# A gated delta-rule memory beside an FFN: crossing the halves for n = 1, and separate PSUM banks

## The chip, the core and the metric

The kernel runs on one core of a Trainium2 chip. The metric is the device time of one execution in microseconds, the median of the runs. A NeuronCore has a matrix engine (TensorE, PE in the profile; its weight loads are PEld), VectorE (DVE), ScalarE (ACT), GpSimd (POOL) and SyncE (SP), which here issues all DMAs. Each works through its own queue in order.

## The reference

The input x has shape [4, 2048, 256]: four batch elements, 2048 tokens, 256 features. A conditioning vector gives, per batch element, two shifts, two scales and two gates (adaLN). Two blocks follow:

```python
h = _layernorm(x) * (1 + ca) + sa
x = x + ga * attn(h)          # gated delta-rule memory, 4 heads of 64, chunks of 64 tokens
h = _layernorm(x) * (1 + cb) + sb
x = x + gb * ffn(h)           # silu(h W1) * (h W2), two GELU layers of 1024, back to 256
```

The memory of a head is a 64x64 state S. For each chunk, with A the inverse of a unit triangular 64x64 matrix that the chunk's keys give:

```python
v_new = A_i @ v_i - (A_i @ wk_i) @ S
o_i = rkg_i @ S + intra_i @ v_new
S = gamma_C * S + wkg_i @ v_new
```

The memory's output is `h + (alpha * o) @ Wr.T`.

## The kernel before

A step is one chunk of 64 tokens of all four batch elements, numbered 2n + b; there are 32 steps. With tokens on partitions, b takes the partitions 64b to 64b + 63 and n lies along the free axis. With features on partitions, head 2p + h takes the partitions 64h to 64h + 63. So the memory's products come in 16 units (p, n, h, b) of 64x64x64, and each of them occupies a 64x64 quarter of the matrix engine: the row half is the partition half of its operands, the column half that of its output.

The FFN of a step runs beside the recurrence of the next step and the chunk's own matrices of the one after that. Its products (line 431) are 128x128 by 256: 128 for the gated layers, 256 for the two hidden layers (16 chunks of 128 outputs, 16 products each), 32 for the last layer. Each activation is kept as two parts, whose sum is exact: `act` is first rounded by ScalarE (L367), and then the residue is computed by VectorE (hidden layers) or GpSimd (gated layers), both L368.

The memory's work in one step, as the matrix engine does it:

- `rec_state` (L305) has two groups of products with the state: R (L310), which is subtracted from v to give `rem`, and O (L314), the part of the memory's output that comes from the state. O stays open in PSUM until `rec_update`.
- the last layer of the FFN (`last`), then the next step's gated layers, and among them the transpositions `tp` (L200);
- `local_grams` (L230): G, the products of keys, masked by VectorE into NMT and IT (L242, L243). NMT's diagonal blocks of 32 go to DRAM (d1) and come back as U in another layout; VectorE inverts them row by row (`local_inverse`, zt and Z, L258 and L260), and `local_blocks` (L263) stores Z to DRAM (d2) and loads it into E by four DMAs; VectorE transposes the blocks into Dm (L271).
- `local_merge1` and `local_merge2` (yp L280, ep L293) complete the inverse E from its blocks of 32;
- `rec_values` (L321): V = E times rem; `rec_update` (L330): IT times vn is added onto the open O in PSUM (L337), SS (L342) updates the state; ScalarE copies O to oT (L345);
- `rec_out` (L353): oT times wrT, the output projection.

The write keys wkg are loaded by two to four DMAs that follow E's loads in SyncE's queue, and GpSimd scales them (L214).

[...] three for the FFN (`pf`), two tiles of two banks each for `ps2`, one for `ps1`. In `ps2` live tp, G, R, O and SS, in `ps1` vp, yp, ep, V, the output projection and a transposition.

The order of each engine's queue is set by a planner that runs through the program with its own estimate of every instruction's duration, and takes what is ready first, what is emitted earlier first. `tc.issue_after` puts the memory's products behind a given FFN product: after the q-th chunk of the hidden layers (`steps`, L658 to L708). The two hidden layers' chunks, q = 0 to 15, are thus the rail along which everything else is placed. The inverse of step s + 2 is spread over these chunks, and `local_blocks` and `rec_state` follow after the 16th.

Set-up (L470 to L646) loads and rounds the weights, compares them with what was rounded (L526, L528), and works out the first matrices. `held` and `after` delay instructions there behind marked ones.

Of the kernel before, what the change touches and what calls it, by code (L numbers as in the profile page):

```python
# [35 lines left out]
# Columns of the constants: what stays, then what only the set-up needs.  # L36
IDENT, UNIT = 0, 128
KEPT = 128 + 8 * K
# [4 lines left out]
def constants():  # L43
    """By the shapes alone: indices and masks over the positions of a tile."""
# [5 lines left out]
    # Row 4 * n + (partition // 32) of the identity.  # L50
    unit = np.zeros((P, 8, K), np.float32)
    for n in range(8):
        unit[i, n, 4 * n + i // K] = 1.0
    out[:, UNIT:UNIT + 8 * K] = unit.reshape(P, -1)
# [7 lines left out]
def over(ap, dim, n):  # L62
    """`ap` with a dimension of n that repeats it."""
    shape = list(ap.shape)
    shape.insert(dim, n)
    return ap.unsqueeze(dim).to_broadcast(shape)
# [3 lines left out]
def adaln_block_kernel(ctx: ExitStack, tc: tile.TileContext, x_in, ww, wr, decay, log_alpha, w1, w2, h1, h2, w3, scol,  # L70
# [17 lines left out]
    kept = cp.tile([P, KEPT], F32, name="kept")  # L88
    ident = kept[:, IDENT:IDENT + P]
    unit = kept[:, UNIT:UNIT + 8 * K].rearrange("q (c i) -> q c i", i=K)  # L90
    wwT = cp.tile([P, NK, D], F32, name="wwT")
    wrT = cp.tile([P, NK, D], F32, name="wrT")
# [47 lines left out]
    def after(name):  # L140
        """What follows is issued behind what was marked last, on its engine."""
        return tc.issue_after(mark[name])
# [15 lines left out]
    def moments(x):  # L158
        """The mean of each token, and one over its deviation."""
# [34 lines left out]
    def local_keys(s, first=False):  # L194
# [7 lines left out]
        nc.scalar.copy(hT, tp[:, 0])  # L202
# [6 lines left out]
        # The write keys, a token behind, with tokens on partitions.  # L209
# [20 lines left out]
    def local_grams(s):  # L230
        IT, NMT = ITs[s % 2], NMTs[s % 2]
        # The heads h are row tiles, each with a bank of its own.
# [18 lines left out]
        nc.gpsimd.tensor_scalar(Z, unit, 1.0, None, ALU.mult)  # L251

    def local_inverse(s, j0, j1):
        """Rows of the inverse of the diagonal blocks of 32: partition (g, block, unit), row 4 * c + g at c."""
# [8 lines left out]
    def local_blocks(s):  # L263
        dst = d2.rearrange("(c g) x u i -> g (x u) c i", g=4)
        for g in range(4):
            move(out=dst[g], in_=Z[K * g:K * g + K])
        for b in range(2):
            for k in range(2):
                r = slice(C * b + K * k, C * b + K * k + K)
                move(out=E[r, :, K * k:K * k + K], in_=d2[:, 2 * b + k])  # L270
        nc.vector.transpose(Dm, E[:, :, 0:K])  # L271

    # E = [[EA, EA NMT EB], [0, EB]], of the blocks of 32.
    def local_merge1(s):
        NMT = NMTs[s % 2]
        yp = ps1.tile([P, 8, K], F32, tag="a1", name="yp")
        for u in range(8):
            for b in range(2):
                a = C * b
# [462 lines left out]
```

## Time and profile before

| | |
|---|---|
| median of three runs | 1785.5 us (1785.21 to 1786.7) |
| span of the profiled execution | 1783.4 us |
| mean granted TensorE clock | 0.983 |
| length of a steady step | 52.5 us |
| busy, PE / DVE / ACT / POOL | 97% / 65% / 55% / 34% |
| products of the FFN (L431), busy | 1024.8 + 256.2 + 126.8 us |
| V (L325), O from the state (L314), busy | 37.6 us (x1024), 36.4 us (x992) |
| R (L310), G (L239), O from vn (L337), SS (L342), busy | 22.3, 22.7, 22.7, 21.1 us |
| yp (L280), ep (L293), busy | 22.2, 22.6 us |

The page gives the span of one profiled execution, from its first to its last instruction, and no other time of that execution; the runs' median is 2.1 us above it. Busy times of a group leave out overlaps. Instructions of the matrix engine are pipelined: the time that one costs the engine is best read from when the next one starts. An fp32 product leaves two records, so 16 units are "x32". In a timeline a row is: start in us, busy us, engine, line, operation, output <- inputs, shapes, count, and in brackets the idle time before it and what ended it. SPq rows are the DMA issues of SyncE.

### The profile page before, as it was taken

To read this page: it belongs to the slowest core of one execution; us is meant where nothing else is said; L and a number is where in the kernel's file an instruction comes from. 1 tells how busy PE (TensorE), PEld (TensorE's weight loads), DVE (VectorE), ACT (ScalarE), POOL (GpSimd) and SP (SyncE) were. 2 spreads that over 40 slices of the span, in tenths; PEclk is the share of its full clock that TensorE was granted. 3 is DMA by queue.
4 is the path that set the end of the run, shared out by engine and by line. 5 is a ranking of instruction groups with operands and counts; after the bars stand their busy time and mean duration, and the time that the engine had idled before them with its cause. 6 is when DMAs were issued, how large, how long until landed. Compare 5 with 4: busy or idle time off the path is not lost.

```text
span 1783.4 us, 49902 instructions
## 1 busy us (share of the span) xinstructions
PE 1724.5 (97%) x20372; PEld 1653.5 (93%) x20372; DVE 1162.4 (65%) x3705; ACT 984.0 (55%) x2254; POOL 615.2 (34%) x615
## 2 busy tenths in 40 slices
PE   6489999999999999999999999999999999999998
PEld 3279999999999999999999999999999999999998
DVE  6876767666767666677766667766667776566532
ACT  6245555565555556555656655555655565565554
POOL 3234323334433334442323443333343232344111
PEclk8689999999999999999999999999999999999999
DMA  8311111111111111111111111111111111111100
GB/s 278 98 40 38 27 29 30 39 40 40 28 30 32 31 40 41 40 25 28 31 38 40 40 29 31 34 28 40 40 40 25 28 32 37 41 40 23 24 2 15
DMA packets 142319, 71.93 MB, mean 40 GB/s; under 512 B 112320, under 2 KB 130624, under 8 KB 142080
## 3 DMA queue, kind: packets, MB, share of 16 engines
q1 hardware_dynamic: 142080, 68.65, 15.9%
q8 instruction: 161, 2.64, 0.6%
q14 instruction: 78, 0.64, 0.1%
HBM read 43.44 MB, written 16.78 MB: 34 GB/s over the span
## 4 chain that ended last, share of the span: by engine, by line
PE 88%; DVE 6%; DMA 3%; SPq 1%; issue 1%; POOL 1%; ACT 0%; POOLq 0%; DVEq 0%; ACTq 0%
PE ps L431 70%; PE vp L224 3%; PE V L325 2%; DVE zt L258 2%; DVE Z L260 2%; PE O L314 2%; PE tp L200 1%; SPq L145 1%; PE G L239 1%; PE yp L280 1%; PE O L337 1%; PE R L310 1%; PE ep L293 1%; PE SS L342 1%; PE tpf L382 1%
## 5 line engine op out<-in xcount | busy, mean ns | idle before, releaser
L431 PE MATMUL ps<-act,fh 128*128 128x256 f32 x8192 | 1024.8, 282 | 2.5 <-DVE raw L442 2.2
L431 PEld LDWEIGHTS ps<-act,fh 128*128 128x128 f32 x8192 | 980.1, 188 | 13.6 <-DVE raw L442 2.6
L450 ACT ACTIVATE raw<-ps,sc 128x256 f32<-128x256 f32 x512 | 244.4, 479 | 369.4 <-PE ps L431 322.8
L368 DVE TENSOR_TENSOR act<-raw,act 128x256 fp32r<-128x256 f32 x512 | 234.2, 471 | 170.3 <-ACT act L367 170.2
L367 ACT CAST act<-raw 128x256 fp32r<-128x256 f32 x768 | 311.1, 406 | 34.2 <-DVE raw L442 21.4
L258 DVE TENSOR_TENSOR zt<-Z,U 128x60 f32<-128x60 f32 (+24 forms) x992 | 244.3, 246 | 92.6 <-DMA U<-d 65.8
L431 PE MATMUL ps<-hs,fw 128*128 128x256 f32 x2048 | 256.2, 282 | 5.6 <-DVE raw L442 4.2
L362 POOL TENSOR_TENSOR y<-y,ga 128x512 f32<-128x512 f32 x32 | 41.1, 1284 | 614.9 <-DVE ga L361 614.9
L431 PEld LDWEIGHTS ps<-hs,fw 128*128 128x128 f32 x2048 | 246.3, 189 | 6.8 <-DVE raw L442 4.8
L260 DVE TENSOR_TENSOR Z<-Z,zt 128x60 f32<-128x60 f32 (+24 forms) x992 | 211.5, 213 | 24.2 <-DVE zt L258 0.6
L442 DVE SCALAR_TENSOR_TENSOR raw<-ps,sc,sg 128x256 f32<-128x256 f32 x256 | 123.7, 483 | 153.5 <-ACT sg L441 149.5
L441 ACT ACTIVATE sg<-ps,sc 128x256 f32<-128x256 f32 x256 | 121.9, 476 | 165.8 <-PE ps L431 164.4
L368 POOL TENSOR_TENSOR act<-raw,act 128x256 fp32r<-128x256 f32 x256 | 187.1, 738 | 58.8 <-ACT act L367 42.6
L431 PE MATMUL ps<-fw,act 128*128 128x256 f32 x1024 | 126.8, 281 | 1.2 <-DVE act L368 0.6
L431 PEld LDWEIGHTS ps<-fw,act 128*128 128x128 f32 x1024 | 120.0, 188 | 3.6 <-DVE act L368 0.8
L167 POOL TENSOR_TENSOR rs<-rs,half 128x2 f32<-128x2 f32 x64 | 54.3, 849 | 114.5 <-DVE rs L166 114.5
L386 ACT ACTIVATE hm<-tpf,modT 128x64 f32<-128x64 f32 x256 | 82.4, 417 | 9.7 <-PE tpf L382 9.7
L214 POOL TENSOR_TENSOR wkg<-wkg,gtail 128x512 f32<-128x512 f32 x32 | 33.5, 1047 | 149.5 <-DMA wkg<-rk 105.8
L224 PE MATMUL vp<-wwT,hT 128*128 128x256 f32 x256 | 63.0, 391 | 15.9 <-DVE modT L626 15.4
L191 POOL TENSOR_TENSOR gh<-hid,mod 128x512 f32<-128x512 f32 x32 | 47.4, 1482 | 77.1 <-DVE rn L182 77.0
L464 DVE TENSOR_TENSOR gb<-ps,mod 128x512 f32<-128x512 f32 (+1 forms) x33 | 22.3, 675 | 77.3 <-PE ps L431 77.3
L224 PEld LDWEIGHTS vp<-wwT,hT 128*128 128x128 f32 x256 | 47.8, 196 | 22.0 <-issue 15.5
(208 smaller groups left out, 1640.2 us busy)
## 6 DMA issues: line engine op xcount, KB each, us to landing
U<-d SPq DMA_DIRECT2D x128, 128.0 KB, 2.5
y<-in_x_dram SPq DMA_DIRECT2D x64, 128.0 KB, 9.3
st<-in_h_dram SPq DMA_DIRECT2D x16, 512.0 KB, 5.6
wkg<-rk SPq DMA_DIRECT2D x64, 126.0 KB
out_dram<-y SPq DMA_DIRECT2D x62, 128.0 KB, 2.5
d<-NMT SPq DMA_DIRECT2D x128, 32.0 KB, 4.2
d<-Z SPq DMA_DIRECT2D x128, 32.0 KB, 1.7
E<-d SPq DMA_DIRECT2D x128, 32.0 KB, 2.0
```

The costliest lines, as they stand in the source:

```text
L167: nc.gpsimd.tensor_tensor(rs, rs, half[:, 0:2], ALU.pow)
L191: nc.gpsimd.tensor_tensor(t, h, mod[:, GA], ALU.mult)
L224: nc.tensor.matmul(vp[:, n, :], lhsT=hT[:, k, n, :], rhs=wwT[:, k, :], start=k == 0, stop=k == NK - 1)
L258: nc.vector.tensor_tensor(t[:, 0:n, 0:w], Z[:, 0:n, j:j + 1].to_broadcast([P, n, w]), over(U[:, j, j + 1:K], 1, n), ALU.mult)
L260: mark["inverse"] = nc.vector.tensor_tensor(Z[:, 0:n, j + 1:K], Z[:, 0:n, j + 1:K], t[:, 0:n, 0:w], ALU.add).ins
L367: nc.scalar.copy(to[0], a)
L368: (eng or nc.vector).tensor_tensor(to[1], a, to[0].bitcast(F32), ALU.subtract)
L386: nc.scalar.activation(hm[:, k, b, :], tp[:, k, b // 2, C * (b % 2):C * (b % 2) + C], AF.Identity, bias=modT[:, k, b:b + 1], scale=modT[:, ...
L431: self.end = nc.tensor.matmul(ps, lhsT=wk if lhs_is_w else a, rhs=a if lhs_is_w else wk, start=k == 0 and i == 0, stop=k == k_n - 1 and i ...
L441: nc.scalar.activation(sg, ps[:, 0, :], AF.Silu, scale=sc[:, 0, o:o + 1])
L442: nc.vector.scalar_tensor_tensor(to, ps[:, 1, :], sc[:, 1, o:o + 1], sg, ALU.mult, ALU.mult)
L450: nc.scalar.activation(to, ps[:, 0, :], AF.Gelu, scale=sc[:, 2 + layer, o:o + 1])
```

## The change

For n = 1 several things lie on the other half of the partitions than before. The inverse E, and what it multiplies (R, and with it v and rem), lie by the other token half: unit (n, b) is at 64 (b xor n). To have v there, hT's token halves are swapped for n = 1. The memory's outputs (O, oT) lie by the other head half: 64 (h xor n); the projection takes for n = 1 a second copy of wrT with its head halves swapped. The inverse's own loads and transpositions follow: eight loads of E instead of four, three transpositions into Dm instead of one.

The parts that belong to n = 0 and n = 1 get PSUM banks of their own in yp, O and V, which are now in `ps2`. O is no longer left open: its part from the state is copied to oT right away by ScalarE, and the part from vn is written to a new tile (`new`, which also holds SS) and added to oT by VectorE. The constants lose the table `unit`; Z is set by five memsets. In set-up `local_grams(1)` goes behind the first `rec_update`. All comments and docstrings are gone in the changed file.

```diff
@@ constants
-IDENT, UNIT = 0, 128
-KEPT = 128 + 8 * K
+IDENT = 0
+KEPT = 128
@@ local_keys
-        nc.scalar.copy(hT, tp[:, 0])
+        nc.scalar.copy(hT[:, :, 0, :], tp[:, 0, :, 0, :])
+        nc.scalar.copy(hT[:, :, 1, :].rearrange("q p (b t) -> q p b t", t=C)[:, :, ::-1, :],
+                       tp[:, 0, :, 1, :].rearrange("q p (b t) -> q p b t", t=C))
@@ local_grams
-        nc.gpsimd.tensor_scalar(Z, unit, 1.0, None, ALU.mult)
+        nc.gpsimd.memset(Z, 0.0)
+        diag = Z.rearrange("q c i -> q (c i)")
+        for g in range(4):
+            nc.gpsimd.memset(diag[K * g:K * g + K, g::K + 4], 1.0)
@@ local_blocks
+        E4, D4 = (t.rearrange("q (a n) i -> q a n i", n=2) for t in (E, Dm))
         for b in range(2):
             for k in range(2):
-                r = slice(C * b + K * k, C * b + K * k + K)
-                move(out=E[r, :, K * k:K * k + K], in_=d2[:, 2 * b + k])
-        nc.vector.transpose(Dm, E[:, :, 0:K])
+                for n in range(2):
+                    r = slice(C * (b ^ n) + K * k, C * (b ^ n) + K * k + K)
+                    move(out=E4[r, :, n, K * k:K * k + K],
+                         in_=d2[:, 2 * b + k].rearrange("j (a n) i -> j a n i", n=2)[:, :, n, :])
+        nc.vector.transpose(D4[:, :, 0, :], E4[:, :, 0, 0:K])
+        for b in range(2):
+            nc.vector.transpose(D4[C * b:C * b + K, :, 1, :], E4[C * (1 - b):C * (1 - b) + K, :, 1, 0:K])
@@ local_merge1
-        yp = ps1.tile([P, 8, K], F32, tag="a1", name="yp")
+        yp = ps2.tile([P, 2, 512], F32, tag="a2", name="yp")
         for u in range(8):
             for b in range(2):
-                a = C * b
-                nc.tensor.matmul(yp[a + K:a + C, u, :], lhsT=NMT[a:a + K, u, K:C], rhs=Dm[a:a + K, u, :],
+                a, e, n, m = C * b, C * (b ^ u % 2), u % 2, u // 2 * K
+                nc.tensor.matmul(yp[e + K:e + C, n, m:m + K], lhsT=NMT[a:a + K, u, K:C], rhs=Dm[a:a + K, u, :],
                                  start=True, stop=True)
...
+    BY_NH = [(p, n, h, b) for p in range(2) for b in range(2) for n in range(2) for h in range(2)]
+    BY_NB = [(p, n, h, b) for p in range(2) for h in range(2) for n in range(2) for b in (1, 0)]
@@ rec_state
-            nc.tensor.matmul(R[C * b:C * b + C, h, m:m + C], lhsT=keys[r, p, n, b, 0:C], rhs=S[r, b, 2 * p + n, :],
+            e = C * (b ^ n)
+            nc.tensor.matmul(R[e:e + C, h, m:m + C], lhsT=keys[r, p, n, b, 0:C], rhs=S[r, b, 2 * p + n, :],
                              start=True, stop=True)
-        for p, n, h, b in UNITS:
-            r, m = slice(C * h, C * h + C), (2 * p + n) * C
-            nc.tensor.matmul(O[r, b, m:m + C], lhsT=S[r, b, 2 * p + n, :], rhs=rkg[r, p, n, b, :],
-                             start=p == 0 and n == 0, stop=False, skip_group_check=True)
+        for p, n, h, b in BY_NH:
+            r, o, m = slice(C * h, C * h + C), C * (h ^ n), (2 * p + b) * C
+            nc.tensor.matmul(O[o:o + C, n, m:m + C], lhsT=S[r, b, 2 * p + n, :], rhs=rkg[r, p, n, b, :],
+                             start=True, stop=True)
+        oT = ap.tile([P, 4, 2, C], F32, tag="oT", name="oT")
+        nc.scalar.copy(oT.rearrange("q (p n) b t -> q n p (b t)", n=2),
+                       O[:, :, 0:256].rearrange("q n (p c) -> q n p c", p=2))
@@ rec_values
-        V = ps1.tile([P, 2, D], F32, tag="a1", name="V")
-        for p, n, h, b in UNITS:
-            q, u = slice(C * b, C * b + C), 4 * h + 2 * p + n
-            nc.tensor.matmul(V[q, n, at(p, h)], lhsT=E[q, u, :], rhs=r[q, n, at(p, h)], start=True, stop=True)
+        V = ps2.tile([P, 2, 512], F32, tag="a2", name="V")
+        for p, n, h, b in BY_NB:
+            q, e, u = slice(C * b, C * b + C), C * (b ^ n), 4 * h + 2 * p + n
+            nc.tensor.matmul(V[q, n, at(p, h)], lhsT=E[e:e + C, u, :], rhs=r[e:e + C, n, at(p, h)],
+                             start=True, stop=True)
@@ rec_update
+        new = ps2.tile([P, 2, 2, 256], F32, tag="a2", name="new")
+        OI, SS = new[:, :, 0, :], new[:, :, 1, :]
         for p, n, h, b in UNITS:
-            q, u, m = slice(C * b, C * b + C), 4 * h + 2 * p + n, (2 * p + n) * C
-            nc.tensor.matmul(O[C * h:C * h + C, b, m:m + C], lhsT=vn[q, n, at(p, h)], rhs=IT[q, u, :],
-                             start=first and p == 0 and n == 0, stop=True, skip_group_check=True)
-        SS = ps2.tile([P, 2, 512], F32, tag="a2", name="SS")
+            q, o, u, m = slice(C * b, C * b + C), C * (h ^ n), 4 * h + 2 * p + n, (2 * p + n) * C
+            nc.tensor.matmul(OI[o:o + C, b, m:m + C], lhsT=vn[q, n, at(p, h)], rhs=IT[q, u, :], start=True, stop=True)
...
-        oT = ap.tile([P, 4, 2, C], F32, tag="oT", name="oT")
-        nc.scalar.copy(oT.rearrange("q m b t -> q b m t"), O[:, :, 0:256].rearrange("q b (m t) -> q b m t", t=C))
+        new4 = OI.rearrange("q b (m t) -> q m b t", t=C)
+        if oT is None:
+            oT = ap.tile([P, 4, 2, C], F32, tag="oT", name="oT")
+            nc.vector.tensor_copy(oT, new4)
+        else:
+            nc.vector.tensor_tensor(oT, new4, oT, ALU.add)
@@ set-up
-        move(out=wrT, in_=wr.rearrange("(k p) o -> p k o", p=P))
+        move(out=wrT[:, 0], in_=wr.rearrange("(k p) o -> p k o", p=P))
+        for h in range(2):
+            move(out=wrT[C * (1 - h):C * (1 - h) + C, 1], in_=wr.rearrange("(k h p) o -> h p k o", h=2, p=C)[h])
...
-                nc.vector.tensor_scalar(wrT[:, p, :], wrT[:, p, :], alc[:, p:p + 1], None, ALU.mult)
+                for n in range(2):
+                    nc.vector.tensor_scalar(wrT[:, n, p, :], wrT[:, n, p, :], alc[:, n, p:p + 1], None, ALU.mult)
...
-        with held("inverse"):
+        oT = rec_update(0, vn, None)
+        with after("updated"):
             local_grams(1)
-        rec_out(0, rec_update(0, vn, None))
+        rec_out(0, oT)
```

More of the change, by code (lines that the diff above doesn't have):

```diff
@@ L49, in constants @@
     out[:, IDENT:IDENT + P] = np.eye(P)
[L51 to L54, printed above, removed]
     out[:, DIFF:DIFF + C] = np.maximum(col - t, 0)
@@ L89, in adaln_block_kernel @@
     ident = kept[:, IDENT:IDENT + P]
-    unit = kept[:, UNIT:UNIT + 8 * K].rearrange("q (c i) -> q c i", i=K)
     wwT = cp.tile([P, NK, D], F32, name="wwT")
-    wrT = cp.tile([P, NK, D], F32, name="wrT")
+    wrT = cp.tile([P, 2, NK, D], F32, name="wrT")
     sc = cp.tile([P, 4, NH], F32, name="sc")
@@ L284, in local_merge1 @@
             r = slice(C * b + K, C * b + C)
-            nc.scalar.copy(Y[r], yp[r])
+            nc.scalar.copy(Y.rearrange("q (a n) i -> q n a i", n=2)[r],
+                           yp[r, :, 0:4 * K].rearrange("q n (a i) -> q n a i", i=K))
         return Y
@@ L318, in rec_state @@
                                 R[:, :, 0:256].rearrange("q h (m e) -> q h m e", e=C), ALU.subtract)
-        return rem, O
+        return rem, oT
     def rec_values(s, r):
-        V = ps1.tile([P, 2, D], F32, tag="a1", name="V")
-        for p, n, h, b in UNITS:
-            q, u = slice(C * b, C * b + C), 4 * h + 2 * p + n
-            nc.tensor.matmul(V[q, n, at(p, h)], lhsT=E[q, u, :], rhs=r[q, n, at(p, h)], start=True, stop=True)
-        vn = ap.tile([P, 2, D], F32, tag="vn", name="vn")
@@ L327, in rec_values @@
-        nc.scalar.copy(vn, V)
-        return vn
-    def rec_update(s, vn, O):
-        wkg, IT = wkgs[s % 2], ITs[s % 2]
-        first = O is None
-        if first:
-            O = ps2.tile([P, 2, 512], F32, tag="a2", name="O")
-        for p, n, h, b in UNITS:
-            q, u, m = slice(C * b, C * b + C), 4 * h + 2 * p + n, (2 * p + n) * C
-            nc.tensor.matmul(O[C * h:C * h + C, b, m:m + C], lhsT=vn[q, n, at(p, h)], rhs=IT[q, u, :],
-                             start=first and p == 0 and n == 0, stop=True, skip_group_check=True)
-        SS = ps2.tile([P, 2, 512], F32, tag="a2", name="SS")
+        V = ps2.tile([P, 2, 512], F32, tag="a2", name="V")
@@ new lines, in rec_values, with rec_update @@
+        for p, n, h, b in BY_NB:
+            q, e, u = slice(C * b, C * b + C), C * (b ^ n), 4 * h + 2 * p + n
+            nc.tensor.matmul(V[q, n, at(p, h)], lhsT=E[e:e + C, u, :], rhs=r[e:e + C, n, at(p, h)],
+                             start=True, stop=True)
+        vn = ap.tile([P, 2, D], F32, tag="vn", name="vn")
+        nc.scalar.copy(vn, V[:, :, 0:D])
+        return vn
+    def rec_update(s, vn, oT):
+        wkg, IT = wkgs[s % 2], ITs[s % 2]
+        new = ps2.tile([P, 2, 2, 256], F32, tag="a2", name="new")
+        OI, SS = new[:, :, 0, :], new[:, :, 1, :]
+        for p, n, h, b in UNITS:
+            q, o, u, m = slice(C * b, C * b + C), C * (h ^ n), 4 * h + 2 * p + n, (2 * p + n) * C
+            nc.tensor.matmul(OI[o:o + C, b, m:m + C], lhsT=vn[q, n, at(p, h)], rhs=IT[q, u, :], start=True, stop=True)
@@ L340, in rec_update @@
         for p, n, h, b in UNITS:
             q, m = slice(C * b, C * b + C), (2 * p + n) * C
-            nc.tensor.matmul(SS[C * h:C * h + C, b, m:m + C], lhsT=wkg[q, n, at(p, h)], rhs=vn[q, n, at(p, h)],
-                             start=True, stop=True)
-        oT = ap.tile([P, 4, 2, C], F32, tag="oT", name="oT")
-        nc.scalar.copy(oT.rearrange("q m b t -> q b m t"), O[:, :, 0:256].rearrange("q b (m t) -> q b m t", t=C))
+            mark["updated"] = nc.tensor.matmul(SS[C * h:C * h + C, b, m:m + C], lhsT=wkg[q, n, at(p, h)],
+                                               rhs=vn[q, n, at(p, h)], start=True, stop=True).ins
@@ L357, in rec_out @@
             for p in range(2):
-                nc.tensor.matmul(ap_[:, n, :], lhsT=oT[:, 2 * p + n].rearrange("q b t -> q (b t)"), rhs=wrT[:, p, :],
+                nc.tensor.matmul(ap_[:, n, :], lhsT=oT[:, 2 * p + n].rearrange("q b t -> q (b t)"), rhs=wrT[:, n, p, :],
                                  start=p == 0, stop=p == 1)
@@ L548, in adaln_block_kernel @@
         lgc = su.tile([P, 2], F32, name="lgc")
-        alc = su.tile([P, 2], F32, name="alc")
+        alc = su.tile([P, 2, 2], F32, name="alc")
         for h in range(2):
@@ L602, in adaln_block_kernel @@
                 r = slice(C * h, C * h + C)
-                nc.vector.tensor_copy(alc[r, :], dec[r, 1, :].rearrange("q (p h) -> q h p", h=2)[:, h, :])
+                for n in range(2):
+                    nc.vector.tensor_copy(alc[r, n, :], dec[r, 1, :].rearrange("q (p h) -> q h p", h=2)[:, h ^ n, :])
             nc.scalar.activation(alc, alc, AF.Exp)
@@ L627, in adaln_block_kernel @@
             for p in range(2):
-                nc.vector.tensor_scalar(wrT[:, p, :], wrT[:, p, :], alc[:, p:p + 1], None, ALU.mult)
+                for n in range(2):
+                    nc.vector.tensor_scalar(wrT[:, n, p, :], wrT[:, n, p, :], alc[:, n, p:p + 1], None, ALU.mult)
             local_residual(0, hid0)
```

## The prediction

> **What bounds the kernel now.** I read the page's first part, then its chain of waits, then the timeline of one steady step, engine by engine.
>
> ```profile
> span 1783.4 us, 49902 instructions
> PE 1724.5 (97%) x20372; PEld 1653.5 (93%) x20372; DVE 1162.4 (65%) x3705; ACT 984.0 (55%) x2254; POOL 615.2 (34%) x615
> ...
> PE 88%; DVE 6%; DMA 3%; SPq 1%; issue 1%; POOL 1%; ACT 0%; POOLq 0%; DVEq 0%; ACTq 0%
> ```
>
> TensorE is busy 97% of the span and holds 88% of the chain. In the stretch from 640 to 692.5 us, one step of 52.5 us, it is busy for all 52.5. So a nanosecond less on TensorE is a nanosecond off the time, as long as nobody makes it wait. TensorE's timeline of that step (start, busy us):
>
> ```profile
> 682.40 0.69 PE L310 MATMUL R<-S,keys 64*64 64x64 f32 x32
> 682.92 1.15 PE L314 MATMUL O<-rkg,S 64*64 64x64 f32 x32
> 684.00 3.92 PE L431 MATMUL ps<-fw,act 128*128 128x256 f32 x32
> ...
> 696.20 0.70 PE L239 MATMUL G<-keys 64*64 64x65 f32 x32
> 696.82 0.69 PE L280 MATMUL yp<-Dm,NMT 32*32 32x32 f32 x32
> 697.45 3.79 PE L431 MATMUL ps<-act,fh 128*128 128x256 f32 x31
> ```
>
> Read the starts: R hands over after 0.52 us, O, as many products of the same size, after 1.08. R uses all four 64x64 quarters of the array, O two. The single records say why: R's start in fours, 7 ns apart, a new four each 58 ns; O's and V's (L325, 705.16 to 706.23, 1.07 us) in twos, also each 58 ns. A quarter takes one record in 58 ns, whatever the others do. (An fp32 product leaves two records.)
>
> The other engines have slack, but not much. VectorE, SyncE and GpSimd around the same moment:
>
> ```profile
> 677.70 0.18 DVE L260 TENSOR_TENSOR Z<-Z,zt 128x8 f32<-128x8 f32 x1
> 678.01 1.79 DVE L368 TENSOR_TENSOR hs<-hm,hs 128x512 fp32r<-128x512 f32 x1
> 679.73 1.93 DVE L368 TENSOR_TENSOR act<-raw,act 128x256 fp32r<-128x256 f32 x3
> 683.79 0.45 DVE L271 STREAM_TRANSPOSE Dm<-E 128x256 f32<-128x256 f32 x1 [2.13 <-DMA E<-d]
> 684.15 0.72 DVE L368 TENSOR_TENSOR act<-raw,act 128x256 fp32r<-128x256 f32 x2
> ```
>
> ```profile
> 677.90 1.81 SPq L145 DMA_DIRECT2D d<-Z  x4
> 680.98 1.82 SPq L145 DMA_DIRECT2D E<-d  x4
> 683.17 1.61 SPq L145 DMA_DIRECT2D wkg<-rk  x2
> ```
>
> ```profile
> 687.22 1.04 POOL L214 TENSOR_TENSOR wkg<-wkg,gtail 128x512 f32<-128x512 f32 x1 [4.85 <-DMA wkg<-rk]
> 688.73 1.29 POOL L465 TENSOR_TENSOR y<-y,gb 128x512 f32<-128x512 f32 x1 [0.46 <-DVE gb L464]
> 690.62 0.74 POOL L368 TENSOR_TENSOR act<-raw,act 128x256 fp32r<-128x256 f32 x1 [0.60 <-PE tp L200]
> ```
>
> VectorE stands still for 2.13 us before the transposition Dm, waiting for a load of E. Behind it in its queue are the last two residues `act` (chunks 14 and 15 of the second hidden layer), which ScalarE had ready at 682.0 and 683.4. The last layer needs them: its 14th product (index 13) at 684.00 + 13 x 0.118 = 685.53, its 16th at 685.77. They are done at 684.5 and 684.87, so this standstill is free today by 0.9 us. In all, Dm waits 64.5 us for E in 32 steps.
>
> **The change part by part, for a step.**
>
> *O.* Four quarters in turn. Priced by the neighbour that does just this and also hands over to the FFN (SS, L342, 709.88 to 710.46): 0.58 instead of 1.08, 0.50 saved, 31 times: 15.5 us.
>
> *V.* Also four quarters; by G (0.62 with the hand-over) instead of 1.07: 0.45 x 32 = 14.4 us.
>
> [...] In the new O and V each bank n is still written by both row tiles (on different partitions). [...] The row: V of before has both row tiles in its single bank, and they start 6 to 7 ns apart. I go by the row[...].
>
> *yp.* 32x32 products, now on two tiles, then on four. Records come in twos each 32 ns. With four tiles 32 x 32 / 4 = 0.26 us instead of 0.51: 0.24 saved, between 0 (if 16 ns a record were an issue limit; R's 7 ns say no) and 0.25: 7.7 us. The merge's second half (ep) is as before.
>
> *Losses on TensorE.* The new product OI crosses its output halves for n = 1, but keeps its order, so at each change of n two quarters come again after two records: 13 + 56 = 69 ns for a four instead of 58, eight fours, 0.09. R likewise 62.5 against 58: 0.04. Over the run 2.9 + 1.2 us. Sum on TensorE: 15.5 + 14.4 + 7.7 - 4.1 = **33.5 us less**, 1.06 a step.
>
> *ScalarE.* oT is copied at the end of the step before (0.59, as L345 now), where ScalarE idles 4.14 us; hT's copy becomes two (2 x 0.36 by the 128x256 copies of set-up, for 0.59): +0.13, under gaps of 0.17 in each chunk. vn and Y keep their sizes. Nothing, and 0.1 if uncovered.
>
> *VectorE.* OI and the old part are now added there: 128x512 from PSUM with an SBUF operand, priced by ga (L361), 0.68. It falls into the inverse (zt, Z), where VectorE has no gap from 705.74 to 730, so the last Z is 0.68 later. Dm becomes three transpositions: one of 128x128 and two of 32x128; 0.445 was 128x256, so about 0.25 + 0.2 + 0.2.
>
> *GpSimd.* Z's copy (0.9) becomes five memsets; a 128x512 one takes 0.52 in set-up, so 0.3 + 4 x 0.1: nothing. It waits for the store of Z as now.
>
> *SyncE.* E is loaded by 8 DMAs instead of 4, of half the size. Each costs its issue: 0.49 us from one to the next. [...] by the SyncE row it costs 4 x 0.49 = 1.96 for what is queued behind (the two wkg loads), and I take the row. For Dm: the diagonal blocks now come with the 1st, 2nd, 5th and 6th load, where the 3rd was the last (issued 681.83, landed 683.69, Dm at 683.79). The 6th: 681.83 + 3 x 0.49 = 683.30, landing 1.86 later, 685.16. [...]
>
> *Set-up.* Four more E loads (+2.0), wrT's loads 1 to 3, two more scalings (0.34 each) and two more copies (0.16), V at the slow clock (1.9) about 0.9 faster, and G of step 1 goes from 42.2 us to behind SS (83.8): its masks (1.36), stores and loads then end some 3 us later than U's use at 91.5. In between VectorE has other work (comparisons). I take +3, between 0 and +6.
>
> **Where the stall goes.** On the clock of before: Z 0.68 later, 6th load 685.16 + 0.68 + 0.1 = 685.94, transposition to 686.1, then a residue (0.36): 686.5. The 16th product wants it at 685.77: **+0.7 a step, and the whole gain on TensorE is lost as well**, since the layer is then set by this chain (G, masks, U, Z, E, Dm, residue) and no longer by TensorE. If both residues stay behind Dm it is +1.1; if only the transposition of the 5th load is ahead of the residue, +0.2. What decides is the planner's order. It put Dm between chunks 13 and 14 in all steady steps: it expects E before chunk 14. E now comes later by some 1 to 2 us in its plan, and TensorE earlier by 1; a chunk is 1.9 us. So Dm most likely slips behind chunk 14, not behind 15. I take +0.4 x 30 steps (those with a step s + 2) = 12 us.
>
> **Rivals.**
>
> 1. *Likeliest: the residue waits behind Dm.* 1785.5 + 12 + 3 = **1800**; own range 1789 to 1815 (0.2 and 1.0 a step). For: the 2.13 us standstill, 0.9 slack. Against: the order may change.
> 2. *Other sign: Dm slips behind both residues,* and TensorE stays the bound: 1785.5 - 33.5 + 3 = **1755**. It decides as soon as Dm stands behind chunk 15. For: VectorE idles 2.4 us right after (before gb), so a later Dm costs nothing, and yp needs it 12 us later.
> 3. *As 2, but GpSimd becomes late.* Its wkg would start at 687.22 + 0.68 + 1.96 = 689.86; y (1.29), a residue (0.74), rkg (1.2) and seven residues queue behind: 690.9 + 1.29 + 0.74 + 1.2 + 5.2 = 699.3, wanted by the first hidden product at 697.45 + 15 x 0.118 = 699.2 on the old clock. So no gain at all: about **1788**; 1765 if y goes ahead of wkg.
> 4. *The change doesn't do it:* [...] only yp gains: 7.7 - 4.1 = 3.6; 1785.5 - 3.6 + 3 = **1785**.
>
> **How the numbers follow.** The sum is made on the profiled span, 1783.4; the page gives no time around it, the median of the runs is 2.1 us above, and I carry that over. Chances: rival 1 0.46, 2 0.31, 3 0.16, 4 0.07. 0.2% (3.6 us, about what a measurement of this kernel can tell): slower 0.44 + 0.09 + 0.02 = 0.55; within 0.02 + 0.05 + 0.04 = 0.11; faster 0.31 + 0.02 + 0.01 = 0.34. Range 1752 to 1812: it takes in rival 2 and the most of 1.
>
> **What would show it.** Right on TensorE: O and V in fours, about 0.6 us each, yp 0.4. Right on the stall: TensorE idle before or in the last layer, released by VectorE's act, and VectorE's wait for E grown from 2.1 to 3 or more with a residue directly behind Dm. If Dm stands behind all residues and a step takes about 51.5 us, rival 2 is right; TensorE idle at the first hidden products, released by GpSimd's act, shows rival 3; O and V still at 1.07, rival 4. I would be wrong altogether if set-up grew by more than 10 us, or if VectorE's collisions with GpSimd (hs 1.79 here, 0.69 alone) fell otherwise, worth 1.1 us each.

## The result, and the profile after

The changed kernel takes 1938.7 us (median of 4 runs, 1933.7 to 1942.5) against 1785.4 us: 1.086 times the time before, 95% interval 1.084 to 1.088. The profiled execution has a span of 1940.7 us, and the mean granted clock of TensorE fell from 0.983 to 0.949. The page's first and fourth parts:

```profile
span 1940.7 us, 50390 instructions
PE 1765.1 (91%) x20372; PEld 1676.6 (86%) x20372; DVE 1190.2 (61%) x3805; ACT 985.6 (51%) x2285; POOL 595.5 (31%) x743
...
DVE 43%; PE 26%; DMA 13%; SPq 11%; issue 4%; ACT 1%; POOL 0%; DVEq 0%; ACTq 0%; POOLq 0%
```

TensorE has the same number of instructions, 91% busy instead of 97, and holds 26% of the chain instead of 88: the chain through VectorE, SyncE and the DMAs now sets the time. And TensorE's busy time grew by 40.6 us, although three groups of its products became shorter. TensorE's timeline of one steady step shows both:

```profile
699.02 0.45 PE L290 MATMUL yp<-Dm,NMT 32*32 32x32 f32 x32
...
707.11 0.69 PE L344 MATMUL V<-rem,E 64*64 64x64 f32 x32
...
737.87 0.65 PE L330 MATMUL O<-rkg,S 64*64 64x64 f32 x32
738.45 1.74 PE L452 MATMUL ps<-fw,act 128*128 128x256 f32 x13
742.58 0.50 PE L452 MATMUL ps<-fw,act 128*128 128x256 f32 x2 [2.39 <-DVE act L389]
744.53 3.52 PE L452 MATMUL ps<-fw,act 128*128 128x256 f32 x17 [1.45 <-DVE act L389]
```

From start to next start, O takes 0.58 us, V 0.63, yp 0.38 (medians of the steady steps; before 1.08, 1.08 and 0.62): the gains are there. Then the last layer stands still twice, 2.39 and 1.45 us, first for the residue of chunk 14, then for that of chunk 15, and the 17 products that are left take 3.5 us, where they took 2.0. The windows view (from:to, length, busy time of PE, PEld, DVE, ACT, POOL, granted clock, DMA share, GB/s) says why:

```profile
738.00:744.50 6.50, 2.69 (x51) 2.22 (x43) 1.79 (x6) 2.25 (x3) 0.73 (x5) 1.00 0.21 43
744.50:748.00 3.50, 3.47 (x18) 3.47 (x19) 0.66 (x2) 0.00 (x0) 1.04 (x1) 0.59 0.12 37
748.00:752.00 4.00, 4.00 (x35) 4.00 (x34) 1.66 (x3) 2.11 (x6) 2.04 (x2) 0.93 0.11 25
752.00:760.00 8.00, 8.00 (x125) 7.75 (x124) 4.09 (x8) 6.84 (x17) 6.22 (x8) 1.00 0.27 64
```

After the standstill the granted clock is 0.59, then 0.93, then 1.00 again. In the trace's clock records this is a stretch of 3.41 us (in some steps 6.83) at half clock, and each of the 28 steady steps (from the fourth G to the last) has one. Before, there was none between set-up and the last step.

Why the residues are late is on VectorE, GpSimd and SyncE (the three timelines of the same step):

```profile
730.06 1.26 DVE L181 TENSOR_SCALAR rn<-rn 128x8 f32<-128x8 f32 x1
...
733.20 1.16 DVE L263 TENSOR_TENSOR zt<-Z,U 128x8 f32<-128x8 f32 x1
734.40 0.97 DVE L265 TENSOR_TENSOR Z<-Z,zt 128x8 f32<-128x8 f32 x1
735.29 0.68 DVE L389 TENSOR_TENSOR hs<-hm,hs 128x512 fp32r<-128x512 f32 x1
735.89 1.08 DVE L389 TENSOR_TENSOR act<-raw,act 128x256 fp32r<-128x256 f32 x3
741.77 0.30 DVE L281 STREAM_TRANSPOSE Dm<-E 32x128 f32<-32x128 f32 x1 [4.80 <-DMA E<-d]
742.10 0.42 DVE L389 TENSOR_TENSOR act<-raw,act 128x256 fp32r<-128x256 f32 x1
743.13 0.31 DVE L279 STREAM_TRANSPOSE Dm<-E 128x128 f32<-128x128 f32 x1 [0.60 <-DMA E<-d]
743.72 0.30 DVE L281 STREAM_TRANSPOSE Dm<-E 32x128 f32<-32x128 f32 x1 [0.28 <-DMA E<-d]
744.05 0.42 DVE L389 TENSOR_TENSOR act<-raw,act 128x256 fp32r<-128x256 f32 x1
```

```profile
729.77 1.51 POOL L189 TENSOR_TENSOR gh<-hid,mod 128x512 f32<-128x512 f32 x1 [2.44 <-DVE rn L180]
...
733.00 1.33 POOL L190 TENSOR_TENSOR y<-y,gh 128x512 f32<-128x512 f32 x1
734.29 1.04 POOL L183 TENSOR_TENSOR rk<-hid,rn 128x512 f32<-128x512 f32 x1
```

```profile
735.39 1.80 SPq L143 DMA_DIRECT2D d<-Z  x4
737.30 0.80 SPq L143 DMA_DIRECT2D wkg<-rk  x1
738.57 4.73 SPq L143 DMA_DIRECT2D E<-d  x8
```

VectorE waits 4.80 us for E in front of the first transposition, with the residue of chunk 14 directly behind it, and that of chunk 15 is behind all three; the order is this in 27 of the 28 steady steps. The last zt and Z of the inverse, operations of 128x8 that took 0.18 before, now take 1.16 and 0.97: they end at 734.36 and 735.37, where GpSimd's y (734.33) and rk (735.33) end. Before, y began beside `hs` (1.79 us), which E does not wait for; `hs` is now back at 0.68. GpSimd before:

```profile
677.96 1.29 POOL L192 TENSOR_TENSOR y<-y,gh 128x512 f32<-128x512 f32 x1
679.21 1.50 POOL L185 TENSOR_TENSOR rk<-hid,rn 128x512 f32<-128x512 f32 x1
```

The medians over 28 steady steps (the fourth to the thirty-first), worked out from both traces, in us from the step's G:

| | before | after | later by |
|---|---|---|---|
| first zt starts | 9.66 | 9.95 | 0.29 |
| last Z ends | 34.01 | 36.68 | 2.67 |
| first load of E is issued | 37.15 | 39.88 | 2.73 |
| last transposition Dm starts | 40.01 | 44.80 | 4.79 |
| last residue (chunk 15) done | 41.10 | 45.55 | 4.45 |
| 16th product of the last layer starts | 42.16 | 45.61 | 3.45 |
| from there to the next G | 10.37 | 12.15 | 1.78 |
| next G | 52.53 | 57.96 | 5.43 |

So the 16th product starts 3.45 us later, by the standstill, and the way from there to the next G, where the half clock falls, is 1.78 us longer (1.96 on average: 2.3 to 2.6 in the eight steps with 6.83 us at half clock). Until the fourth G, 7.3 us are lost (176.9 against 169.6). 7.3 + 28 steps of 5.36 on average make 157.3, the difference of the two spans.

One more delay is in these rows. From E's first load to the last transposition it takes 4.92 us instead of 2.86. Part of that is the four more loads; another part goes with the packets that the page lists as `q8 instruction` (instruction packets below): 161 packets and 2.64 MB in both kernels, each about 1.1 us long. Their number stays at 161 in the run below with four more DMA issues a step, is 162 in the one with the transpositions moved, and 168 in the one with 28 more products a step; that they are TensorE's is the author's estimate from these counts. One of them starts 39.4 to 41.7 us after G in every steady step, in both kernels. Before, E is nearly always through by then: one packet in 28 steps starts while E is under way (from 0.3 us before the first load's issue to 1 us before the last transposition). In the changed kernel, where E is later, it is so in 27 of 28. No run moved these packets alone; what they go with is read from the traces.

### The profile page after: what moved, and what is told of

Its sections match the earlier page's. It is cut to its first block, busy times and chain, and to the rows that moved or that the text cites. A ratio compares the mean times of both kernels' runs of the same rounds, so it can differ in the third digit from the quotient of the medians.

```text
span 1940.7 us, 50390 instructions
## 1 busy us (share of the span) xinstructions
PE 1765.1 (91%) x20372; PEld 1676.6 (86%) x20372; DVE 1190.2 (61%) x3805; ACT 985.6 (51%) x2285; POOL 595.5 (31%) x743
## 3 DMA queue, kind: packets, MB, share of 16 engines
q8 instruction: 161, 2.64, 0.6%
## 4 chain that ended last, share of the span: by engine, by line
DVE 43%; PE 26%; DMA 13%; SPq 11%; issue 4%; ACT 1%; POOL 0%; DVEq 0%; ACTq 0%; POOLq 0%
PE ps L452 23%; DVE zt L263 13%; SPq L143 11%; DVE Z L265 11%; DVE act L389 5%; DMA U<-d 5%; DMA E<-d 3%; DMA d<-NMT 3%; DMA d<-Z 2%; DVE bs L161 2%; DVE rn L181 2%; PE tp L198 1%; DVE hid L173 1%; DVE S L369 1%; DVE rn L180 1%
## 5 line engine op out<-in xcount | busy, mean ns | idle before, releaser
L263 DVE TENSOR_TENSOR zt<-Z,U 128x60 f32<-128x60 f32 (+24 forms) x992 | 271.6, 274 | 111.7 <-DMA U<-d 87.1
L389 DVE TENSOR_TENSOR act<-raw,act 128x256 fp32r<-128x256 f32 x512 | 210.9, 421 | 157.7 <-ACT act L388 155.8
L452 PE MATMUL ps<-hs,fw 128*128 128x256 f32 x2048 | 272.6, 292 | 10.8 <-DVE hs L389 6.4
L452 PEld LDWEIGHTS ps<-hs,fw 128*128 128x128 f32 x2048 | 264.9, 201 | 11.9 <-DVE hs L389 6.9
L452 PE MATMUL ps<-fw,act 128*128 128x256 f32 x1024 | 180.6, 338 | 101.3 <-DVE act L389 100.8
L452 PEld LDWEIGHTS ps<-fw,act 128*128 128x128 f32 x1024 | 159.9, 237 | 115.2 <-DVE act L389 112.4
L265 DVE TENSOR_TENSOR Z<-Z,zt 128x60 f32<-128x60 f32 (+24 forms) x992 | 233.7, 236 | 24.8
L281 DVE STREAM_TRANSPOSE Dm<-E 32x128 f32<-32x128 f32 x64 | 19.3, 301 | 146.1 <-DMA E<-d 144.5
```

The source lines that it names most:

```text
L263: nc.vector.tensor_tensor(t[:, 0:n, 0:w], Z[:, 0:n, j:j + 1].to_broadcast([P, n, w]), over(U[:, j, j + 1:K], 1, n), ALU.mult)
L265: mark["inverse"] = nc.vector.tensor_tensor(Z[:, 0:n, j + 1:K], Z[:, 0:n, j + 1:K], t[:, 0:n, 0:w], ALU.add).ins
L389: (eng or nc.vector).tensor_tensor(to[1], a, to[0].bitcast(F32), ALU.subtract)
L452: self.end = nc.tensor.matmul(ps, lhsT=wk if lhs_is_w else a, rhs=a if lhs_is_w else wk, start=k == 0 and i == 0, stop=k == k_n - 1 and i ...
```

## The experiments

Theory: the late residue of chunk 15, made late by three things (8 loads of E, the collisions of zt and Z with GpSimd, the transpositions ahead of it in VectorE's queue), plus the half clock that follows each standstill. Rivals: the collisions come from elsewhere in the change; the products behind the stall are slow by themselves; the chain would be too long in any order. Every ratio below is to the kernel before on the same chip, 1782.8 to 1784.7 us.

**Transpositions behind the last residue.**

```diff
+        with after("residue") if "residue" in mark else ExitStack():
             nc.vector.transpose(D4[:, :, 0, :], E4[:, :, 0, 0:K])
             ...
```

> The changed kernel, with the three transpositions Dm issued behind the last residue (chunk 15) on VectorE; nothing else differs. Theory 1, the queue: the last layer's 16th product is late only because its residue stands behind Dm in VectorE's queue. Then the stall and what follows it vanish, TensorE is the bound again, and the time is 1785.4 - 33.5 (worked out on TensorE) + 7 (the set-up, read from the two traces) = 1759 us, 1750 to 1770, with the granted clock at 1.00 in the steady steps. Theory 2, the chain: G, masks, U, Z, E, Dm is now too long in itself and its next consumer (the products yp) or GpSimd behind the wkg loads becomes late instead: 1785 or more, with idle time of TensorE at yp or at the first hidden products.

1828.5 us, 1.026 times (1.024 to 1.028). The standstill in the last layer is gone in all 28 steps and with it the half clock. But a step still takes 53.7 us, not 51.5, and the time goes elsewhere. TensorE, and GpSimd just before:

```profile
706.28 0.66 PE L198 MATMUL tp<-kept,hid 128*128 128x128 f32 x4 [0.61 <-DVE rem L337]
...
711.78 1.22 PE L455 MATMUL ps<-hs,fw 128*128 128x256 f32 x8 [0.55 <-DVE raw L466]
713.62 1.21 PE L455 MATMUL ps<-hs,fw 128*128 128x256 f32 x8 [0.62 <-DVE raw L466]
```

```profile
708.22 1.04 POOL L215 TENSOR_TENSOR wkg<-wkg,gtail 128x512 f32<-128x512 f32 x1 [7.19 <-DMA wkg<-rk]
709.22 1.29 POOL L489 TENSOR_TENSOR y<-y,gb 128x512 f32<-128x512 f32 x1
```

Theory 1 is right on the stall; theory 2 is right that something else becomes late behind it: GpSimd waits 7.19 us for a load of wkg that is queued behind the 8 loads of E, and its residues, and so the gated products, come late. Also `rem`, now behind Dm, frees the PSUM tile of tp too late.

**Eight loads of E alone,** in the kernel before.

```diff
-                move(out=E[r, :, K * k:K * k + K], in_=d2[:, 2 * b + k])
+                for n in range(2):
+                    move(out=E.rearrange("q (a n) i -> q a n i", n=2)[r, :, n, K * k:K * k + K],
+                         in_=d2[:, 2 * b + k].rearrange("j (a n) i -> j a n i", n=2)[:, :, n, :])
```

> The kernel before, with E loaded by 8 DMAs of half the bytes instead of 4; Dm stays one transposition of 128x256 and now waits for all 8; in the written order it stands between residues 14 and 15. Theory 1, the SyncE issues push Dm and with it the residue of chunk 15 past the 16th product: the 8th load is issued 4 x 0.49 = 1.96 us later than the 4th, Dm about 2 us later than 683.79, residue at 686.6 against 685.77 wanted: 0.8 us a step of stall, 1785 + 30 x 0.8 = 1809 us if a stall costs its length, and 1809 + 30 x 2 = 1870 if each stall also halves the clock for one 3.4 us window, as the changed kernel's trace looks. Rival, the loads are cheap and the changed kernel's loss came from VectorE alone: 1785 to 1790.

1809.5 us, 1.015 times (1.013 to 1.017): 26 us, the number reckoned without a clock loss, but not in the way reckoned, so the number is luck. Dm did go behind chunk 14. Only 16 of 28 steps have a standstill, of 0.8 to 1.8 us, and they are exactly those in which an instruction packet starts while E is under way: there it takes 4.92 to 5.73 us from E's first load to Dm, in the other 12 3.97 to 4.30. In those 12 the residue comes in time, so there the four more issues cost nothing. The clock stays at 1.00 in all 28; TensorE in a step with a standstill (15 + 17 products, the latter in 2.05 us to the next group's start):

```profile
641.02 1.99 PE L433 MATMUL ps<-fw,act 128*128 128x256 f32 x15
644.33 2.22 PE L433 MATMUL ps<-fw,act 128*128 128x256 f32 x17 [1.31 <-DVE act L370]
646.38 1.98 PE L433 MATMUL ps<-hs,fw 128*128 128x256 f32 x16
```

**The addition alone,** in the kernel before, its result unused.

```diff
         nc.scalar.copy(oT.rearrange("q m b t -> q b m t"), O[:, :, 0:256].rearrange("q b (m t) -> q b m t", t=C))
+        spare = ap.tile([P, 2, D], F32, tag="tmp", name="spare")
+        nc.vector.tensor_tensor(spare, SS[:, :, 0:256], vn, ALU.add)
```

> The kernel before, with one more VectorE addition of 128x512 (PSUM and SBUF operand, result unused) at the place where the changed kernel adds OI: 4 loads of E as before. Theory 1, only its length counts: Z ends 0.68 us later, the residue of chunk 15 still comes 0.2 us before its product: 1785 to 1790 us. Theory 2, it moves the inverse into GpSimd's operations, whose collisions lengthen zt and Z by another 1.8 us a step: the residue is then 1.6 us late, with the clock's window 3.6 us a step, 1785 + 30 x 3.6 = 1890 us.

1880.5 us, 1.054 times (1.051 to 1.056). One operation of 0.68 us a step, whose result nobody reads, costs 97 us. The last Z ends at 36.45 instead of 34.01, with the same rows as in the changed kernel (VectorE, then GpSimd):

```profile
710.80 1.16 DVE L258 TENSOR_TENSOR zt<-Z,U 128x8 f32<-128x8 f32 x1
711.99 0.97 DVE L260 TENSOR_TENSOR Z<-Z,zt 128x8 f32<-128x8 f32 x1
712.89 0.68 DVE L370 TENSOR_TENSOR hs<-hm,hs 128x512 fp32r<-128x512 f32 x1
```

```profile
710.60 1.34 POOL L192 TENSOR_TENSOR y<-y,gh 128x512 f32<-128x512 f32 x1
711.88 1.06 POOL L185 TENSOR_TENSOR rk<-hid,rn 128x512 f32<-128x512 f32 x1
```

That is theory 2 (1890), though the collisions are not all of it: the residue of chunk 15 comes 3.66 us later (44.76), and Z accounts for 2.44. From E's first load to Dm it takes 3.9 us instead of 2.9, with the same four loads, and in 25 of 28 steps an instruction packet starts in that time. The standstills are 2.0 to 3.4 us in all steps but one, and in 13 of 28 half clock follows.

**TensorE kept busy in the standstill,** in the changed kernel.

```diff
                         r, O = rec_state(s + 2)
+                        fill = ps1.tile([P, 512], F32, tag="a1", name="fill")
+                        for i in range(28):
+                            nc.tensor.matmul(fill[:, 0:N], lhsT=fh1[:, i % NH, 0:P], rhs=fh2[:, i % NH, 0:N],
+                                             start=True, stop=True)
                 f.last(0)
```

> The changed kernel, with 28 extra products (128x128 by 128x256, exact weights of the hidden layer, result unused) put on TensorE between O and the last layer, in every step that has a step s + 2; they take 28 x 0.118 = 3.3 us, as long as TensorE stands still there today. Theory 1, the standstill's second cost is the clock: with TensorE kept busy no window of half clock follows, and the 17 products behind the stall take 2.0 us instead of 3.4 to 4.0: 1938.7 - 30 x 1.5 to 2.0 = 1880 to 1895 us. Rival, the products behind the stall are slow for another reason (their operands, their weights): 1939 us or, if the fill overruns, more.

1890.5 us, 1.060 times (1.058 to 1.062): 3.3 us more work a step, and 48 us less time. The residue of chunk 15 comes as late as ever (45.40), but the products behind it run at the full rate, and no half clock is left in the steady steps:

```profile
719.69 3.62 PE L735 MATMUL fill<-fh,fh 128*128 128x256 f32 x28
723.14 1.93 PE L452 MATMUL ps<-fw,act 128*128 128x256 f32 x15
726.07 2.20 PE L452 MATMUL ps<-fw,act 128*128 128x256 f32 x17 [0.99 <-DVE act L389]
728.10 1.99 PE L452 MATMUL ps<-hs,fw 128*128 128x256 f32 x16
```

A step takes 55.96 us instead of 57.96, and from the 16th product to the next G it is 10.50 us, against 12.15 in the changed kernel and 10.37 before. So 1.65 us of the table's 1.78 are the clock (1.83 on average, 51 us in 28 steps).

**The memory outputs alone crossed:** O, OI and wrT as in the change; E, V and yp on the halves of before, V and yp still in their new banks.

```diff
-            e = C * (b ^ n)
+            e = C * b
             nc.tensor.matmul(R[e:e + C, h, m:m + C], lhsT=keys[r, p, n, b, 0:C], rhs=S[r, b, 2 * p + n, :],
...
-            q, e, u = slice(C * b, C * b + C), C * (b ^ n), 4 * h + 2 * p + n
+            q, e, u = slice(C * b, C * b + C), C * b, 4 * h + 2 * p + n
...
+        for b in range(2):
+            for k in range(2):
+                r = slice(C * b + K * k, C * b + K * k + K)
+                move(out=E[r, :, K * k:K * k + K], in_=d2[:, 2 * b + k])
+        nc.vector.transpose(Dm, E[:, :, 0:K])
```

> Only the memory outputs lie crossed (O in four quarters, OI added on VectorE, wrT by the other head half); the matrices E, V and yp lie as before: 4 loads of E, one transposition Dm. Theory 1, the addition on VectorE brings the 2.4 us of collisions into the inverse, as in the kernel before with the bare addition: the last layer waits 2.0 to 3.4 us, half clock follows in some steps, and what TensorE saves at O (0.41 a step after OI's loss) is swallowed by the wait: 1870 to 1890 us. Rival, the addition in its true place (its result wanted by TensorE, other neighbours) falls between GpSimd's operations: 1785 - 12 = 1773 us, up to 1790.

1882.7 us, 1.055 times (1.053 to 1.058), last Z at 36.50. Theory 1: in its true place the addition does the same harm, and O's gain is swallowed. V takes 1.08 us and yp 0.62, as before: their new banks, without the crossed halves, gain nothing.

**The changed kernel without the addition.**

```diff
-            nc.vector.tensor_tensor(oT, new4, oT, ALU.add)
+            pass
```

> The changed kernel without the addition of OI on VectorE, so that its output leaves out what the chunk's own values add to the memory's output; all else as in the changed kernel, the 8 loads of E and the transposition between residues 14 and 15 too. Theory 1, the collisions come from the addition's 0.68 us: the last Z ends 2.4 us earlier, the residue of chunk 15 comes at 43.2 instead of 45.6 us after G, the stall shrinks from 2.5 to under 1.8 us and no half clock follows: 57.96 - 2.4 - 2.0 = 53.6 us a step, 1785 + 1.1 x 30 + 7 = about 1825 us (1805 to 1845). Theory 2, half clock follows even the shorter stalls: about 1885 us. Rival, the collisions come from elsewhere in the change (its earlier TensorE, its three transpositions): 1920 us or more.

1842.9 us, 1.031 times (1.028 to 1.034): 96 us less. The last Z is back at 34.03 (34.01 before). So the addition brought the collisions, and nothing else in the change did. The standstill is 2.0 us in the median, a little longer than expected, and half clock follows in 11 of 28 steps, between the two theories. What is left is E's stretch: 5.2 us to the last transposition, with an instruction packet in it in all 28 steps.

**The collision itself:** the kernel before with the bare addition, and GpSimd's residual (gh, y) behind the reset of Z.

```diff
                         local_grams(s + 2)
+                    with after("reset"):
+                        local_residual(s + 2)
```

> The kernel before with the bare VectorE addition, as in the run that gave 1880 us, and with GpSimd's residual (gh and y, two operations of 128x512) issued behind the reset of Z instead of during the inverse; of GpSimd's 128x512 operations only rk is left beside the inverse. Theory, a VectorE operation that begins while such a GpSimd operation runs ends only when that one ends (rn 1.27 against 0.17 beside gh, zt 1.16 against 0.18 beside y, Z 0.97 against 0.17 beside rk): two of the three stretched operations go back to their own lengths, the last Z ends about 1.9 us earlier, at 34.5 to 35.0 us after G, one of about 0.8 us is left, the stall shrinks to under 0.5 us and no half clock follows: 1785 to 1805 us. Rival, the addition delays the inverse in another way (its own length, its place in the order, the PSUM read): Z ends at 36 or later, 1860 to 1885 us.

1808.3 us, 1.014 times (1.012 to 1.016), against 1880.5 with the same addition. The last Z ends at 34.34. VectorE's operations are as short as alone, except the one that begins beside rk:

```profile
683.64 0.17 DVE L183 TENSOR_SCALAR rn<-rn 128x8 f32<-128x8 f32 x1
...
685.69 0.99 DVE L258 TENSOR_TENSOR zt<-Z,U 128x8 f32<-128x8 f32 x1
686.72 0.18 DVE L260 TENSOR_TENSOR Z<-Z,zt 128x8 f32<-128x8 f32 x1
```

```profile
685.61 1.05 POOL L185 TENSOR_TENSOR rk<-hid,rn 128x512 f32<-128x512 f32 x1
```

The theory of the collision holds. The time is just above what it allowed, because the standstill is 1.1 us and not under 0.5: rk is now ready earlier, both loads of wkg went ahead of those of E, and E is issued 0.9 us later than before (38.09). In 17 steps an instruction packet then starts while E is under way (4.22 us to Dm, in the other 11 3.01). Besides, the planner put Dm behind chunk 14 here, which it had not with the bare addition. So the place of the last Z is what shows the collision; the 72 us between the two runs are not its price alone.

**Towards a version that gains: wkg's loads ahead of E's,** with the transpositions behind the last residue.

```diff
         nc.gpsimd.tensor_tensor(heads(rk), heads(hid), over(rn, 2, C), ALU.mult)
+        if s > 1:
+            write_keys(s)
```

Here `write_keys` holds the loads that `local_keys` issued.

> The changed kernel with the transpositions Dm behind the last residue and both loads of the write keys (wkg) ahead of the 8 loads of E on SyncE's queue. Theory: with Dm out of the way, what still held the step at 53.7 us was GpSimd, whose wkg waited for a load queued behind 8 loads of E (208.2 on GpSimd's row 708.22), so that its residues of the first hidden layer came late by 3 x 0.6 us. With the loads in front, wkg starts some 4 us earlier, those three waits vanish, TensorE is the bound at about 51.5 us a step: 1785 - 33.5 + 5 = 1757 us (1748 to 1765). Rival, the waits are VectorE's own (its products raw) and not GpSimd's: 1815 to 1830 us, as with Dm alone moved.

(The 208.2 in that text is a slip; the row begins at 708.22.) 1799.2 us, 1.008 times (1.007 to 1.010). GpSimd's wkg begins 42.7 us after G instead of 47.1, and TensorE's weight loads wait 4.1 us in all for `raw` instead of 32.7. The waits of tp for `rem` stayed (27.6 us), and the expected 1757 was not reached.

**The same with a better order of R and OI.**

```diff
+    OI_ORDER = [(p, n, h, b) for p in range(2) for n in range(2) for h in (range(2), (1, 0))[n] for b in range(2)]
+    R_ORDER = [(p, n, h, b) for p in range(2) for n in range(2) for h in range(2) for b in (range(2), (1, 0))[n]]
```

> As the run before this one, and R and OI written so that at each change of n a quarter of the array is used again only after four products: by the prediction's terms 0.04 and 0.09 a step less on TensorE, 4 us in all: 1753 us where the run before gives 1757. Rival, the order doesn't matter at that place: the same time within 2 us.

1797.8 us, 1.007 times (1.006 to 1.009): not told apart from the run before it.

**Dm behind `rem` too.**

```diff
                         r, O = rec_state(s + 2)
+                    with after("rem"):
+                        turn_blocks()
```

`turn_blocks` holds the three transpositions; before, they ended `local_blocks`.

> The changed kernel with both wkg loads ahead of the loads of E, as two runs before, and with the transpositions Dm one place further back on VectorE: behind rem, which frees the PSUM tile that the transpositions tp of the next keys want. Theory: the 0.9 us a step that TensorE still waits for rem (49.6 us in 28 steps on its two rows, counted twice) vanish, TensorE is the bound at 51.5 us a step: 1799 - 1.2 x 30 = 1763 us, 1755 to 1768; this would be below the kernel before by 1 to 1.5%. Rival, the next wait takes its place (the copy of the keys behind Dm, GpSimd's residues): 1780 to 1799 us.

1780.6 us, 0.9987 times (0.9975 to 0.9998). The wait for `rem` is gone, but the rival was right that a next one follows: E lands so late that `gb`, which frees a tile of PSUM for the gated products, stands behind Dm (VectorE):

```profile
740.23 0.68 DVE L346 TENSOR_TENSOR rem<-v,R 128x512 f32<-128x512 f32 x1
744.79 0.31 DVE L290 STREAM_TRANSPOSE Dm<-E 128x128 f32<-128x128 f32 x1 [3.88 <-DMA E<-d]
745.13 0.62 DVE L292 STREAM_TRANSPOSE Dm<-E 32x128 f32<-32x128 f32 x2
745.76 0.17 DVE L215 COPY keys<-keys 128x8 f32<-128x8 f32 x1
745.85 0.69 DVE L497 TENSOR_TENSOR gb<-ps,mod 128x512 f32<-128x512 f32 x1
```

A step takes 52.34 us against 52.53; the best ones 51.6.

**That with the order of R and OI.**

> As the run before this one, with R and OI in the order that uses a quarter of the array again only after four products: with TensorE as the bound the prediction's terms 0.04 and 0.09 a step, 4 us, should now show: 1759 us where the run before gives 1763. Rival: no difference over 2 us.

1779.9 us, 0.9978 times (0.9964 to 0.9991), the fastest kernel here, by about as much as can be measured. The order itself shows no difference: R and OI take 0.52 us each in either order, so there was nothing to gain.

**The control: the kernel before with Dm behind the last residue.**

```diff
-        nc.vector.transpose(Dm, E[:, :, 0:K])
+        with after("residue") if "residue" in mark else ExitStack():
+            nc.vector.transpose(Dm, E[:, :, 0:K])
```

> The control: the kernel before with its transposition Dm behind the last residue. Its standstill at Dm is free already, so moving it should bring nothing: 1783 to 1788 us. If moving Dm alone were worth something, the runs on the changed kernel would show that and not the change: under 1780 us.

1783.1 us, 0.9998 times (0.9990 to 1.0007). Before, Dm's standstill really was free.

## Why the prediction was right or wrong

**TensorE: right, and a little better.** 0.58, 0.63 and 0.38 us for O, V and yp against the 0.58, 0.62 and 0.4 worked out. The loss of 4.1 us reckoned for R and OI did not come: each takes 0.52, as before. With what was measured the sum is 37.7 us instead of 33.5. The fourth rival, O and V left at 1.07, did not come: the row of V, whose products start in pairs 6 to 7 ns apart in a single bank, was right, for quarters that lie on different partitions. No run has both row halves write the same partitions of one bank, so whether that would cost anything is not shown.

**The likeliest case: right in kind.** A residue came late behind Dm and the whole gain was lost. In detail it was worse than the 0.7 worked out: the first transposition, on which the long wait falls, stayed ahead of chunk 14, and the other two went between 14 and 15. So both residues were late, for which the prediction had 1.1.

**The step that failed: VectorE's addition, "the last Z is 0.68 later".** It was 2.67 later, to within 0.1 the sum of 0.68 for the addition (its row has 0.683), 0.29 for a later U, and 1.76 for zt and Z (15.75 us a step instead of 13.99), which now meet GpSimd's y and rk. The prediction had the row (`hs` 1.79 instead of 0.69) and named a fall of such collisions elsewhere among what would make it wrong, but gave it no share of the chances and no place in the range. The bare addition, its removal and the moved residual show this cause from three sides. The residue of chunk 15 so came 4.45 us later instead of 1.63, against a slack of 1.06 (0.9 reckoned): 2.67 by Z, 2.06 in E's stretch, 0.06 at its first issue, less 0.34 because the residue now follows the last transposition directly. TensorE, too, waits for the addition, at the output projection: 9.7 us in 18 of the 28 steps, where the prediction had nothing.

**E's stretch: 2.06 longer where 1.47 was reckoned.** The four issues are about 1.1 of it, and what goes with the instruction packet, which the prediction did not have, about 1.0: in the kernel with the standstill filled, which has the same eight loads, the stretch is 4.97 us in 19 steps with a packet and 3.94 in 9 without, against 2.86 before.

**The term that was missing: the clock.** A standstill was priced at its own length. The filled standstill shows about 50 us of the 153 on top (48 by the two medians, 51 by the steps). In the profile of before the granted clock is 1.00 in every steady slice, and the prediction did not ask what a standstill would do to it.

**The averaging "+0.4 x 30": too small,** by the items above. With the measured step of 5.43 us, the same sum gives 1785 + 7 + 28 x 5.43 = 1944; measured 1939. The range "1789 to 1815" is also a few us too low for its own terms: 0.2 and 1.0 a step in 30 steps, with 3 for set-up, make 1794 and 1818.

**Set-up: 7.3 instead of 3,** outside the 0 to 6 given. It is not this pair of profiles alone: up to the fourth G it is 165.7 to 172.2 us in the five profiles of the kernel before and its variants, and 173.8 to 177.3 in those of the changed kernel and its variants, but for the one with the outputs alone (170.3). Its parts were not separated by a run.

**The other-sign rival, Dm behind both residues, 1755: wrong as a forecast.** Run, that order gives 1828.5. What it left out stood in the third rival: GpSimd behind wkg's loads. That one had the right mechanism, but at 1788 it was reckoned too cheaply. With both repaired, and `rem` as well, the time comes to 1780: of what TensorE gains, the set-up takes 7 us, and the rest goes mostly in waits. In the steady steps of the run with Dm behind `rem`, TensorE waits 6.6 us for `gb` and, at the output projection, 5.6 us for oT (its weight loads 10.9 and 9.6); before, it waits for neither. That split was read from the traces, not tested.

## What to carry to other kernels

An operation added to a nearly full engine can cost more than its length when what is behind it shifts into something that it collides with: here 0.68 us a step cost 97 us, with zt at 1.16 us instead of 0.18 beside another engine's operation and E's stretch at 3.9 us instead of 2.9, in 25 of 28 steps with an instruction packet in it. List what the shifted operations and transfers will then meet, and price that as a case of its own. Price a standstill of TensorE with the clock that may follow it (here about 50 us of the 153). A transposition or copy that waits for a DMA belongs behind everything in its engine's queue that is wanted sooner (moving Dm alone brought the changed kernel from 1938.7 to 1828.5 us), and once it is there, the loads behind that DMA have to be followed in the same way (GpSimd then waited 7.19 us for wkg).

## What was not expected of the hardware

**The clock can fall after a standstill of 2 us.** With the standstills of one last layer added up: none of 28 steps with up to 1.8 us was followed by half clock (eight loads alone); of the 84 steps of the three kernels with 0.6 to 3.4 us (bare addition, outputs alone, no addition), 36; of the changed kernel's 28 with 3.4 to 4.8 us, all. Among the 36, the shortest has 1.97 us; among those without, the longest 3.41. So between 1.97 and 3.41 us steps went either way; what decides is not shown. In the changed kernel a stretch at half clock is 3.41 us long in 20 of the 28 steps and 6.83 in eight.

**A short VectorE operation can wait out a long GpSimd one.** zt of 128x8 takes 0.18 us alone and 1.16 beside y, ending within 0.04 us of it; so does rn, 1.26 beside gh and 0.17 without. What makes them wait is not shown.

**SyncE's issues are not all alike.** In the steady part of before, 23 of the 112 issues of wkg took over 0.9 us, 3 of 112 of U and no issue of E; in the changed kernel 19 of 113 of wkg, 14 of 112 of U and 26 of 224 of E (these with a median of 1.37 us, the longest 1.86). All 26 and 59 slow issues have a record of the instruction packets (q8) between 1 us before their start and their end; of the other issues, 11% have. Which transfers are hit is not a matter of their number alone: with the bare addition, which has as many issues as before, 19 of 112 of E are slow. E came later there, into the time of a packet. That the packets hold up SyncE and its transfers is read from these times alone; how they would is not shown.
